# A cosine transform moved from 64x64 to 128x32 column tiles, and transposes written as four 128x32 matmuls, in a block-matching filter kernel

## Chip, cores and metric

The kernel runs on one core of one Trainium2 chip. The metric is the time of one execution on the device in microseconds (us), the median of several runs; less is better. A core has five engines with a queue of instructions each: TensorE (PE in the profile, its weight loads PEld), VectorE (DVE), ScalarE (ACT), GpSimd (POOL) and SyncE (SP). The last two issue most of the DMA transfers here. TensorE reads its operands from SBUF (128 partitions) and writes its results to PSUM, where ScalarE and VectorE pick them up.

## What is computed

The input is x of 8 images, 32 channels, 128 x 128 pixels. Layer 0 normalises x in groups, and finds for each pixel, by block matching in a 5 x 5 window, the 8 offsets with the smallest patch distance. It stacks the 8 shifted copies to 256 channels `xb` (channel = 8 c + k). Layer 1 is a 5 x 5 filter on each channel. Cut to what matters:

```python
xb = _patch_match_stack(x)                 # [8, 256, 128, 128]
dct = _conv(xb, dct_w, groups=C)           # 8 channels in, 8 out, per c
h = relu(_conv(_conv(xb, w1), w2, groups=CK, pad=1))
h = relu(_conv(_conv(h, w3), w4, groups=CK, pad=1))
wiener = sigmoid(_conv(_conv(h, w5), w6, groups=CK, pad=1))
filt = _conv(wiener * dct, inv_dct_w, groups=C)
return _conv(filt, agg_w)
# layer 0: x = x + that(_gn(x));  layer 1: x = x + conv5x5(_gn(x))
```

All data are 32-bit floats. `dct` is the grouped convolution that the change is about: 32 groups of 8 x 8 weights, one product per pixel. It multiplies `wiener` just before the two last 1 x 1 convolutions, which the kernel folds into one matrix `lagg`.

## The kernel before

Each image is cut into 16 strips of 8 rows, and a 17th step finishes the rows that the convolutions' halos left over (136 steps in all). A step runs four stages in the order 3, 2, 1, 0: stages 1 to 3 are the three pairs of a 1 x 1 convolution (`pointwise_v`, `pointwise_t`) and a 3 x 3 depthwise one (`depthwise_v` on VectorE, `depthwise_t` on TensorE), each one strip further behind; stage 0 is the end of a strip: cosine transform, product with `wiener`, `lagg` matmuls (`final_dct`, `final_add`). Between them the step issues a share of the gather for a later strip (`gather_load`, `gather_select`, `gather_pixels`) and of the block matching and statistics of the next image, which wait in the task queues D, A, P, Q and B. How much of the D queue (VectorE's) a step takes is set by costs written into the code (`yield "D", 1.85`) and the function `tick`. The order of instructions on TensorE, VectorE and ScalarE is the order of the program; on GpSimd and SyncE the framework's scheduler puts the transfers into an order of its own when the kernel is built.

What the change and the steps after it touch:

- `final_load` (L770): for strip n it loads four pieces of x (`xr`, L781) and the gathered pixels `xf` back from DRAM (`xbd`, written by L640), all issued by GpSimd. The 256 channels are split over two halves m of 128 partitions. `xf` has one buffer, so its transfers wait until the matmuls of the strip before have read it. The partition order is made by the transfers: eight of them (m, h, g), 32 partitions and 4 KB a row each.
- `mixes` (L300): builds `ldct`, the block-diagonal weights of the cosine transform, [128, 2, 64], from 32 small loads `dq` (L308), once at the start.
- `final_dct` (L796): for each block of four rows (512 columns) and both m, two matmuls with 64 rows of contraction and 64 output partitions each. The four of a block fill the four 64x64 quadrants of the array. Results `pc` lie in two PSUM buffers; VectorE multiplies them into `acc` (L818).
- `ps_x` (L72): a ring of five PSUM buffers, which `pc`, the results of `pointwise_v` (`pv`, L670), `pointwise_t` (`p`, L694), the gather (`pg`, L631), `lagg` (`pa`, L831) and the transposes share. A matmul into a buffer waits until the engine that read it before is done.
- The other large matmuls use 128x32 tiles: 32 output partitions each, four in a row at output partitions 0, 32, 64 and 96 (`pw`, L751, the depthwise stage; `pv`, `p`, `pg`, `pa`). Some use other shapes: the 5 x 5 filter of layer 1 (L924, 64x64), group sums (L255, L264) and the weight preparation (128x128).
- Transposes of 128 x 128 on TensorE with an identity matrix `ident`, in the transpose form of the instruction: `px` in `sources` (L407, 32 per image, before the gather source `xtd` is written by 30 transfers, L424), `pt` in `costs` (L525, 32 per image), `pi` in `places` (L569, 8 per image), and 14 in the setup.
- `gather_load` (L584): GpSimd loads the index rows `ib` (L602), three buffers; ScalarE turns them into selection matrices `sel` (L616, L617) that the `pg` matmuls use.
- `depthwise_v` (L711): eight VectorE instructions per stage and strip (L725), VectorE's largest group.

Of the kernel before, what the change touches and what calls it, by code (L numbers as in the profile page):

```python
# [8 lines left out]
F32 = mybir.dt.float32  # L9
# [7 lines left out]
P = 128  # L17
C, K, H, W = 32, 8, 128, 128
# [18 lines left out]
C_M32 = C_G2 + 32  # L37
# [7 lines left out]
def bm3d_conv_preact(  # L45
# [16 lines left out]
    nc = tc.nc  # L62
    NB = x.shape[0]

    const = ctx.enter_context(tc.tile_pool(name="const", bufs=1))
    keep = ctx.enter_context(tc.tile_pool(name="keep", bufs=1))
    xnp = ctx.enter_context(tc.tile_pool(name="xn", bufs=1))
    work = ctx.enter_context(tc.tile_pool(name="work", bufs=2))
# [29 lines left out]
    cst = const.tile([P, C_N], F32, name="cst")  # L98
    nc.sync.dma_start(cst, consts)
    ident = cst[:, C_ID : C_ID + P]  # L100
# [3 lines left out]
    lw5 = const.tile([P, 2, CK], F32, name="lw5")  # L104


    ldct = const.tile([P, 2, 64], F32, name="ldct")
    lagg = const.tile([P, 2, C], F32, name="lagg")


# [89 lines left out]

    queues = {"B": deque(), "D": deque(), "A": deque(), "P": deque(), "Q": deque()}

# [94 lines left out]
    def mixes():  # L300

        dq = work.tile([P, 2, K], F32, name="dq", tag="dq", bufs=1)
        src = dct_w.rearrange("(m h c i) k a b -> m h k c (i a b)", m=2, h=2, i=K)
        for k in range(K):
            for m in range(2):
                for h in range(2):
                    p = 64 * h + 32 * (k % 2) + 8 * (k // 2)
                    nc.sync.dma_start(dq[p : p + 8, m], src[m, (h + m + 1) % 2, k])  # L308
        m8 = work.tile([P, 8], F32, name="m8", tag="m16", bufs=1)
        yield "D", 1.0, 10  # L310
        nc.vector.tensor_reduce(
            m8,
            cst[:, C_M32 : C_M32 + C].rearrange("p (a c) -> p c a", c=8),
            axis=mybir.AxisListType.X,
            op=ALU.add,
        )
        for m in range(2):
            nc.vector.tensor_tensor(
                ldct[:, m].rearrange("p (c i) -> p c i", i=K),
                m8.unsqueeze(2).to_broadcast([P, 8, K]),  # L320
                dq[:, m].unsqueeze(1).to_broadcast([P, 8, K]),
                ALU.mult,
            )

        iv = work.tile([P, 2, K], F32, name="iv", tag="iv", bufs=1)
        nc.sync.dma_start(iv, inv_w.rearrange("(m p) k a b -> p m (k a b)", p=P))
        ag = work.tile([C, CK], F32, name="ag", tag="xr")
        nc.sync.dma_start(ag, agg_w.rearrange("c i a b -> c (i a b)"))
        for m in range(2):
            yield "D", 0.5  # L330
            ib = work.tile([P, P], F32, name=f"ib_{m}", tag="xm")
            nc.vector.tensor_tensor(
                ib.rearrange("p (c k) -> p c k", k=K),
                cst[:, C_M16 : C_M16 + 16].unsqueeze(2).to_broadcast([P, 16, K]),
                iv[:, m].unsqueeze(1).to_broadcast([P, 16, K]),
                ALU.mult,
            )
            yield "P", 0
            ps = ps_x.tile([P, 512], F32, name=f"ps_ag_{m}", tag="x")[:, :C]
            nc.tensor.transpose(ps, ag[:, m * P : (m + 1) * P], ident[:C, :C])  # L340
            agt = work.tile([P, C], F32, name=f"agt_{m}", tag="agt")
            nc.scalar.copy(agt, ps)
            yield "P", 0
            ps2 = ps_x.tile([P, 512], F32, name=f"ps_ia_{m}", tag="x")[:, :C]
            nc.tensor.matmul(ps2, ib, agt, start=True, stop=True)
            nc.scalar.copy(lagg[:, m], ps2)
# [52 lines left out]
    def sources(b, xn):  # L399


        xl = dram.tile([H, W, C], F32, name=f"xl_{b}", tag="xl")
        for r in range(0, 32, 4):
            yield "P", 0
            pt = ps_x.tile([P, 4, P], F32, name=f"px_{b}_{r}", tag="x")
            for q in range(4):
                nc.tensor.transpose(pt[:, q], xn[:, 3 + r + q, 2 : 2 + W], ident)  # L407
            xs = work.tile([P, 4, P], F32, name=f"xs_{b}_{r}", tag="ct")
            nc.scalar.copy(xs, pt)
            for q in range(4):  # L410
                nc.gpsimd.dma_start(
                    xl.rearrange("(g r) x c -> r x g c", g=4)[r + q],
                    xs[:, q].rearrange("p (g c) -> p g c", c=C),
                )
        xt = xtd[b] = dram.tile([H, QW, NT, C], F32, name=f"xtd_{b}", tag="xtd")
        for j in range(QW):
            for f in range(2):
                ta, tz = f * (NT // 2), (f + 1) * (NT // 2)
                if j < 2 and f == 0:
                    ta += 1  # L420
                if HW * f + TW * (NT // 2 - 1) + j - 2 >= W:
                    tz -= 1
                xa = HW * f + TW * (ta - f * (NT // 2)) + j - 2
                nc.gpsimd.dma_start(  # L424
                    xt[:, j, ta:tz], xl[:, xa : xa + TW * (tz - ta - 1) + 1 : TW]
                )
        jz = W + 2 - HW - TW * (NT // 2 - 1)
        for ja, jz, t, at in ((0, 2, 0, 0), (jz, QW, NT - 1, W - 1)):
            nc.gpsimd.dma_start(
                xt[:, ja:jz, t], xl[:, at : at + 1].to_broadcast([H, jz - ja, C])  # L430
            )
# [53 lines left out]
    def costs(b, i, sq, idx):  # L485
# [35 lines left out]
        for h in range(0, R, 4):  # L521
            yield "P", 0
            pt = ps_x.tile([P, 4, P], F32, name=f"pt_{b}_{i}_{h}", tag="x")
            for q in range(4):
                nc.tensor.transpose(pt[:, q], cost[:, h + q], ident)  # L525
            if h:
                held.clear()
            ct = work.tile([P, 4, P], F32, name=f"ct_{b}_{i}_{h}", tag="ct")
            nc.scalar.copy(ct[:, :, 0 : 4 * NO], pt[:, :, 0 : 4 * NO])
            mx = work.tile([P, 16, K], F32, name=f"mx_{b}_{i}_{h}", tag="mx")  # L530
            for q in range(4):
                yield "D", 1.85
                y = 8 * i + h + q
                for rg in range(4):
                    c25 = ct[:, q, rg : rg + 4 * NO - 3 : 4]
                    nc.vector.max(mx[:, 4 * q + rg], c25)  # L536
                    nc.vector.max_index(  # L537
                        idx[:, rg, y // 4, :, y % 4], mx[:, 4 * q + rg], c25
                    )
        push(places(b, idx, i))  # L540

    def places(b, idx, i):
# [23 lines left out]
        yield "P", 0  # L566
        for h in range(2):
            pt = ps_x.tile([P, 512], F32, name=f"pi_{b}_{i}_{h}", tag="x")
            nc.tensor.transpose(pt[:, :P], o[:, h * P : (h + 1) * P], ident)  # L569
            li = work.tile([P, P], U8, name=f"li_{b}_{i}_{h}", tag="li")  # L570
            nc.scalar.copy(li, pt[:, :P])
            for f in range(2):
                nc.gpsimd.dma_start(
                    idxd[b][i, 4 * h : 4 * h + 4, f],
                    li[:, HW * f : HW * (f + 1)],
                )
# [193 lines left out]
    def final_load(b, n):  # L770
        j0, j1 = (3, R) if n == 0 else (0, R if n < NS else 3)
        ya, yz = R * n - 3 + j0, R * n - 3 + j1

        whole = j1 - j0 == R
        nr, nw = (2, W) if whole else (j1 - j0, C)
        xr = work.tile([P, 2 * W], F32, name=f"xr_{b}_{n}", tag="xr")
        xr = xr[:, : nr * nw].rearrange("p (r w) -> p r w", w=nw)
        for j in range(4):
            ra = ya + 2 * j if whole else ya
            xa = 0 if whole else C * j  # L780
            nc.gpsimd.dma_start(  # L781
                xr[C * j : C * (j + 1)], x[b, :, ra : ra + nr, xa : xa + nw]
            )

        xf = xbp.tile([P, 2, R, W], F32, name=f"xf_{b}_{n}", tag="xf", bufs=1)
        src = xbd[b].rearrange("(j m h c) g y x -> g m h j c y x", j=4, m=2, h=2)
        for m in range(2):
            for h in range(2):
                for g in range(2):
                    p = 64 * h + C * g  # L790
                    nc.gpsimd.dma_start(  # L791
                        xf[p : p + C, m, j0:j1], src[g, m, (h + m + 1) % 2, :, :, ya:yz]
                    )
        return xr, xf, j0, j1

    def final_dct(b, n, acc, xf, j0, j1):  # L796

        for r0 in range(0, R, 4):
# [5 lines left out]
            pc = [  # L804
                ps_x.tile([P, 4, W], F32, name=f"pc_{b}_{n}_{m}_{r0}", tag="x") for m in range(2)
            ]
            for h in range(2):
                for m in range(2):
                    o = 64 * ((h + m + 1) % 2)
                    nc.tensor.matmul(  # L810
                        pc[m][o : o + 64, : z - a],
                        ldct[64 * h : 64 * h + 64, m],
                        xf[64 * h : 64 * h + 64, m, a:z],
                        start=True,
                        stop=True,
                    )
# [362 lines left out]
```

## Time and profile before

| | |
|---|---|
| median of 3 runs | 6524.21 us (6519.26 to 6526.59) |
| the profiled execution: its time | 6526.97 us |
| the profiled execution: first to last instruction (span) | 6525.2 us |
| mean granted TensorE clock | 0.979 of full speed |
| TensorE: `pc` (L810), all forms | 2112 records, 64x64, 128 to 512 columns |
| TensorE: `px`, `pt`, `pi` (L407, L525, L569) | 256, 256 and 64 records, 128x128; 272, 272 and 327 ns median each |
| VectorE: depthwise (L725) | 3264 instructions, 4031.6 us |
| VectorE: `pc` product (L818) | 528 instructions, 679 ns median |
| GpSimd: issues of `xf` (L791) | 1088, 651.0 us, 632 ns each; 180.6 us of waiting for `pc` before them |
| GpSimd: issues of `ib` (L602) | 512, 570 ns each; 1207.3 us of waiting before them |
| from issue to landing, median | `xf` of 128 KB 6.8 us, `ib` 4.0 us |

How to read it: an engine's share of busy time is a mean over stages with different limits. TensorE's records overlap: the next matmul starts while the last one's results still run out, so four records of 590 ns in four column tiles occupy the array together for about 430 ns, and the time that a row of matmuls takes is read from start to start. An fp32 matmul leaves two records (two passes), a transpose one. The chain of waits is followed back from the last instruction; where it passes through an engine, that engine's work set the time there. What the profile calls a line is the line of the program that issued the instruction.

### The profile page before, as it was taken

How to read it: one execution, taken by the hardware profiler on the slowest of the kernel's cores; microseconds unless marked ns; L12 is line 12 of the kernel's file. 1: busy time of each engine (PE TensorE's matmuls, PEld its weight loads, DVE VectorE, ACT ScalarE, POOL GpSimd, SP SyncE). 2: the span in 40 equal slices, each digit the busy share in tenths (PEclk: the TensorE clock that was granted, in tenths of full speed). 3: DMA queues.
4: the chain of work that ended last, by engine and by line, in shares of the span. 5: the costliest groups of instructions: out<-in, count | busy, mean ns of one | idle time of the engine just before them, and what ended most of it. 6: DMA issues, size and time to landing. Idle time of an engine off the chain costs nothing.

```text
span 6525.2 us, 234180 instructions
## 1 busy us (share of the span) xinstructions
PE 6180.3 (95%) x102306; PEld 3262.3 (50%) x102306; DVE 5856.5 (90%) x8828; ACT 5051.0 (77%) x6698; POOL 3077.3 (47%) x5015
## 2 busy tenths in 40 slices
PE   5799999999999999999999999999999999999997
PEld 1445445544555546454555544544545454465553
DVE  7899988999889998899998999899998999988776
ACT  5787769778787877877778787887869787787772
POOL 8345436444364444643446534454345644344334
PEclk7899999999999999999999999999999999999998
DMA  4555555565555655655546556565555665455553
GB/s 85 125 135 144 123 124 146 145 143 135 133 145 139 142 147 127 150 140 135 141 129 157 140 131 151 127 150 137 139 134 138 150 147 133 118 149 147 137 135 79
DMA packets 544960, 886.21 MB, mean 136 GB/s; under 512 B 248880, under 2 KB 312944, under 8 KB 543936
## 3 DMA queue, kind: packets, MB, share of 16 engines
q0 software_dynamic: 383648, 611.87, 37.4%
q1 hardware_dynamic: 157776, 258.11, 16.4%
q8 instruction: 805, 13.19, 0.9%
q10 hardware_dynamic: 2512, 1.25, 0.1%
q14 instruction: 219, 1.79, 0.1%
HBM read 420.60 MB, written 216.49 MB: 98 GB/s over the span
## 4 chain that ended last, share of the span: by engine, by line
PE 50%; DVE 32%; ACT 5%; POOL 5%; DMA 4%; issue 4%; SPq 0%; ACTq 0%; DVEq 0%; POOLq 0%
DVE acc L725 21%; PE pw L751 16%; PE pv L670 12%; PE p L694 11%; PE pg L631 4%; DVE idx L537 3%; POOL xtd L424 3%; PE pc L810 2%; DVE df L444 2%; DVE acc L818 1%; PE p L924 1%; DVE mx L536 1%; PE pd L459 1%; DMA t<-t 1%; ACT sel L616 1%
## 5 line engine op out<-in xcount | busy, mean ns | idle before, releaser
L725 DVE SCALAR_TENSOR_TENSOR acc<-tv,dwv,acc 128x1024 f32<-128x1024 f32 (+3 forms) x3264 | 4031.6, 1237 | 156.3 <-ACT acc L722 52.0
L751 PE MATMUL pw<-t,dwd 96*32 96x254 f32 (+7 forms) x31680 | 2118.1, 419 | 23.0 <-DMA t<-t 10.1
L751 PEld LDWEIGHTS pw<-t,dwd 96*32 96x32 f32 (+1 forms) x31680 | 1105.7, 110 | 826.8 <-issue 369.3
L616 ACT ACTIVATE sel<-ib,nplace 128x1024 f32<-128x1024 uint8 x1024 | 1170.8, 1143 | 62.0 <-DMA ib<-idxd 62.0
L617 ACT ACTIVATE sel<-sel 128x1024 f32<-128x1024 f32 x1024 | 1086.0, 1061 | 32.5
L670 PE MATMUL pv<-acc,lw 128*32 128x512 f32 x8448 | 959.8, 590 | 54.4 <-DVE acc L818 47.8
L694 PE MATMUL p<-acc,lw 128*32 128x256 f32 x16768 | 974.3, 379 | 2.2 <-issue 2.2
L602 POOL DMA_DIRECT2D ib<-idxd x512 | 292.0, 570 | 1207.3 <-ACT sel L616 1078.1
L791 POOL DMA_DIRECT2D xf<-xbd x1088 | 651.0, 632 | 279.9 <-PE pc L810 180.6
L694 PEld LDWEIGHTS p<-acc,lw 128*32 128x32 f32 x16768 | 570.7, 111 | 393.6 <-issue 67.4
L729 ACT ACTIVATE acc<-acc 128x1024 f32<-128x1024 f32 (+3 forms) x408 | 417.1, 1022 | 390.2 <-DVE acc L725 389.8
L678 ACT COPY tv<-pv 128x512 f32<-128x512 f32 (+2 forms) x784 | 435.9, 579 | 338.5 <-PE pv L670 334.1
L631 PE MATMUL pg<-sel,xt 120*32 120x88 f32 (+1 forms) x24576 | 611.7, 244 | 64.8 <-ACT sel L617 56.1
L631 PEld LDWEIGHTS pg<-sel,xt 120*32 120x32 f32 x24576 | 559.5, 111 | 219.2 <-ACT sel L617 74.4
L670 PEld LDWEIGHTS pv<-acc,lw 128*32 128x32 f32 x8448 | 290.2, 110 | 532.3 <-issue 409.7
L764 ACT ACTIVATE acc<-pw 128x512 f32<-128x512 f32 (+2 forms) x808 | 436.6, 572 | 133.4 <-PE pw L751 131.8
L444 DVE TENSOR_TENSOR df<-xn 128x786 f32<-128x786 f32 (+2 forms) x576 | 530.4, 972 | 2.2 <-PE pd L459 1.9
L701 ACT COPY t<-p 128x512 f32<-128x512 f32 x800 | 421.7, 571 | 115.4 <-PE p L694 115.4
L452 ACT ACTIVATE df<-df 128x786 f32<-128x786 f32 (+2 forms) x576 | 458.9, 859 | 50.0 <-DVE df L444 48.6
L722 ACT ACTIVATE acc<-tv,dwv 128x1024 f32<-128x1024 f32 (+3 forms) x408 | 455.1, 1115 | 42.3 <-PE pa L831 24.8
L670 PE MATMUL pv<-xb,lw 128*32 128x512 f32 x4096 | 470.8, 596 | 0.0
L694 PE MATMUL p<-xb,lw 128*32 128x256 f32 x8192 | 469.9, 380 | 0.0
(155 smaller groups left out, 5893.0 us busy)
## 6 DMA issues: line engine op xcount, KB each, us to landing
ib<-idxd POOLq DMA_DIRECT2D x512, 256.0 KB, 4.0
xbd<-xb POOLq DMA_DIRECT2D x128, 1024.0 KB, 6.0
xf<-xbd POOLq DMA_DIRECT2D x960, 128.0 KB, 6.8
t<-t SPq DMA_DIRECT2D x792, 128.0 KB
t<-t SPq DMA_DIRECT2D x384, 256.0 KB
tv<-tv SPq DMA_DIRECT2D x384, 130.0 KB
xt<-xtd POOLq DMA_DIRECT2D x240, 180.0 KB, 4.0
xtd<-xl POOLq DMA_DIRECT2D x192, 96.0 KB, 3.3
```

What stands on the lines that cost most here:

```text
L444: nc.vector.tensor_sub(df[:, :, ca:cz], xn[:, r0 : r0 + SR, ca:cz], xn[:, r0 + dy : r0 + dy + SR, ca + dx : cz + dx],)
L452: nc.scalar.activation(df[:, :, ca:cz], df[:, :, ca:cz], AF.Square)
L616: nc.scalar.activation(sel, ib, AF.Square, bias=nplace)
L617: nc.scalar.activation(sel, sel, AF.Relu, scale=-1.0, bias=1.0)
L631: nc.tensor.matmul(pg[C * j : C * (j + 1), :, :, xa:xz], xt[: 8 * QW, f * (NT // 2) + t], sels[j // 2][: 8 * QW, j % 2 * 2 : j % 2 * 2 + 2 ...
L670: nc.tensor.matmul(ps[C * j : C * (j + 1), :hr], lhsT[:, g, P + C * j : P + C * (j + 1)], src(g)[:, h : h + hr], start=g == 0, stop=g == 1,)
L694: nc.tensor.matmul(ps[C * r : C * (r + 1), e, :nb], lhsT[:, g, s], rows[:, r : r + 4 * nb - 3 : 4], start=g == 0, stop=g == 1,)
L722: nc.scalar.activation(acc, rows, AF.Copy, scale=tap)
L725: nc.vector.scalar_tensor_tensor(acc, rows, tap, acc, op0=ALU.mult, op1=ALU.add)
L751: nc.tensor.matmul(pt[u][C * j : C * (j + 1), ka:kz, :nb, xa:xz], dwd[0:hi, i - 1, u, j, dx + 1], t[0:hi, j, ka:kz, :nb, xa + dx : xz + dx ...
L764: nc.scalar.activation(rows[:, u : u + 2 * nh[u] - 1 : 2, :nb], pt[u][:, : nh[u], :nb], funcs[i - 1])
L791: nc.gpsimd.dma_start(xf[p : p + C, m, j0:j1], src[g, m, (h + m + 1) % 2, :, :, ya:yz])
```

## The change

`ldct` becomes 128 columns wide per half, and its partition order becomes the natural one (j, c, g) of `xbd`, so that `xf` arrives by two transfers of 128 partitions instead of eight of 32. `final_dct` issues eight matmuls per block, each with all 128 rows and 32 output partitions, of which most weights are zeros: an output tile q uses the columns 32 q to 32 q + 32 of `ldct`. All transposes of `px`, `pt` and `pi` go through a new function that issues four ordinary matmuls of 128x32, with the data as weights and the identity as the moving operand. The transposes of the setup stay.

```diff
-    ldct = const.tile([P, 2, 64], F32, name="ldct")
+    ldct = const.tile([P, 2, P], F32, name="ldct")
...
+    def transpose(out_, in_):
+        for j in range(0, P, C):
+            nc.tensor.matmul(out_[j : j + C], in_[:, j : j + C], ident, start=True, stop=True)
...
-        src = dct_w.rearrange("(m h c i) k a b -> m h k c (i a b)", m=2, h=2, i=K)
+        src = dct_w.rearrange("(m c i) k a b -> m k c (i a b)", m=2, i=K)
         for k in range(K):
             for m in range(2):
-                for h in range(2):
-                    p = 64 * h + 32 * (k % 2) + 8 * (k // 2)
-                    nc.sync.dma_start(dq[p : p + 8, m], src[m, (h + m + 1) % 2, k])
-        m8 = work.tile([P, 8], F32, name="m8", tag="m16", bufs=1)
+                p = 32 * (k // 2) + k % 2
+                nc.sync.dma_start(dq[p : p + 31 : 2, m], src[m, k])
+        m16 = work.tile([P, 16], F32, name="m16", tag="m16", bufs=1)
...
-            cst[:, C_M32 : C_M32 + C].rearrange("p (a c) -> p c a", c=8),
+            cst[:, C_M32 : C_M32 + C].rearrange("p (c g) -> p c g", g=2),
...
-                m8.unsqueeze(2).to_broadcast([P, 8, K]),
-                dq[:, m].unsqueeze(1).to_broadcast([P, 8, K]),
+                m16.unsqueeze(2).to_broadcast([P, 16, K]),
+                dq[:, m].unsqueeze(1).to_broadcast([P, 16, K]),
...
-                nc.tensor.transpose(pt[:, q], xn[:, 3 + r + q, 2 : 2 + W], ident)
+                transpose(pt[:, q], xn[:, 3 + r + q, 2 : 2 + W])
...
-                nc.tensor.transpose(pt[:, q], cost[:, h + q], ident)
+                transpose(pt[:, q], cost[:, h + q])
...
-            nc.tensor.transpose(pt[:, :P], o[:, h * P : (h + 1) * P], ident)
+            transpose(pt[:, :P], o[:, h * P : (h + 1) * P])
...
-        src = xbd[b].rearrange("(j m h c) g y x -> g m h j c y x", j=4, m=2, h=2)
+        src = xbd[b].rearrange("(j m c) g y x -> m j (c g) (y x)", j=4, m=2)
         for m in range(2):
-            for h in range(2):
-                for g in range(2):
-                    p = 64 * h + C * g
-                    nc.gpsimd.dma_start(
-                        xf[p : p + C, m, j0:j1], src[g, m, (h + m + 1) % 2, :, :, ya:yz]
-                    )
+            nc.gpsimd.dma_start(
+                xf[:, m, j0:j1].rearrange("p y x -> p (y x)"), src[m, :, :, W * ya : W * yz]
+            )
...
-            for h in range(2):
-                for m in range(2):
-                    o = 64 * ((h + m + 1) % 2)
+            for m in range(2):
+                for q in range(4):
+                    s = slice(C * q, C * (q + 1))
                     nc.tensor.matmul(
-                        pc[m][o : o + 64, : z - a],
-                        ldct[64 * h : 64 * h + 64, m],
-                        xf[64 * h : 64 * h + 64, m, a:z],
+                        pc[m][s, : z - a],
+                        ldct[:, m, s],
+                        xf[:, m, a:z],
```

## The prediction

> **What bounds the kernel now.** I read the page's shares and chain first, then TensorE's timeline in a late stretch, then busy times of single steps, then the chain where GpSimd appears in it.
>
> ```profile
> span 6525.2 us, 234180 instructions
> PE 6180.3 (95%) x102306; PEld 3262.3 (50%) x102306; DVE 5856.5 (90%) x8828; ACT 5051.0 (77%) x6698; POOL 3077.3 (47%) x5015
> ...
> PE 50%; DVE 32%; ACT 5%; POOL 5%; DMA 4%; issue 4%; SPq 0%; ACTq 0%; DVEq 0%; POOLq 0%
> ```
>
> TensorE is nearly full, VectorE almost as full, and the chain changes sides between them. So work added to TensorE costs its full length in some steps and nothing in others. The change adds TensorE work, and the question is how many steps pay.
>
> The price comes from one step of the last image (start, start to end, form, records; each fp32 matmul leaves two records):
>
> ```profile
> 6220.44 1.04 PE L751 MATMUL pw<-t,dwd 128*32 128x508 f32 x8
> 6221.41 1.95 PE L810 MATMUL pc<-xf,ldct 64*64 64x512 f32 x16
> 6223.29 1.16 PE L631 MATMUL pg<-sel,xt 120*32 120x88 f32 x48
> ...
> 6229.42 3.62 PE L670 MATMUL pv<-acc,lw 128*32 128x512 f32 x32
> 6232.85 1.06 PE L831 MATMUL pa<-acc,lagg 128*32 128x256 f32 x16
> 6233.72 3.65 PE L694 MATMUL p<-acc,lw 128*32 128x256 f32 x64
> 6237.17 1.14 PE L631 MATMUL pg<-sel,xt 120*32 120x88 f32 x48
> 6238.12 3.62 PE L670 MATMUL pv<-acc,lw 128*32 128x512 f32 x32
> ```
>
> Ends overlap the next start, so I count from start to start. 32 records of 128x32 by 512 columns take 6232.85 - 6229.42 = 3.43 us (107 ns each, four column tiles side by side), 64 records by 256 columns 6237.17 - 6233.72 = 3.45 (54 ns), 48 by 88 columns 6238.12 - 6237.17 = 0.95 (20 ns). The cosine product takes 6223.29 - 6221.41 = 1.88 us for 16 records; its four 64x64 tiles also run together. It is entered late: the eight `pw` records should take 8 x 0.107 = 0.85 and take 0.97.
>
> **The cosine product.** A full strip has two blocks of four rows. Before: 0.97 + 1.88 = 2.85 us from the `pw` records to `pg`. After: eight matmuls per block, 32 records of exactly the `pv` form, so 0.85 + 3.43 = 4.28. That is +1.43 us per strip, the vanished changes of tile shape already in it: the records' own price rises by 1.72 (16 x 107 ns) and about 0.28 of entry and exit goes. The first strip of an image has 640 columns instead of 1024 and the last 384, which gives +0.8 and +0.36. An image pays 15 x 1.43 + 1.2 = 22.7, eight images 182 us of TensorE time, 1.33 per strip on average.
>
> The page "TensorEngine Tiling (Array Packing)" of the Trainium skill speaks against the change: under Theoretical Speedup it gives up to 2x where a dimension is at most 64, and the change fills the rows up to 128 with zeros. By that rule the product would take 2 x 1.88 = 3.76 us instead of the 3.43 that the `pv` rows give, and the sum would be, as an estimate, 45 us larger if all 136 strips paid; the rows decide, because the 1.88 holds the entry and exit that go.
>
> **Who pays.** I cut the trace at each strip's first `pc` record into 135 steps and took TensorE's time without streaming (gaps over 0.16 us, so that changes of shape do not count) and VectorE's idle time in each. Three steps, one of each kind (sum and mean of the answer left out):
>
> ```profile
> core 0: us, PE busy (x) PEld busy (x) DVE busy (x) ACT busy (x) POOL busy (x), PEclk, DMA share, GB/s
> 6221.40:6264.20 42.80, 42.80 (x758) 23.11 (x754) 33.99 (x31) 34.93 (x44) 12.60 (x23) 1.00 0.53 137
> 3868.70:3916.00 47.30, 45.09 (x773) 22.01 (x772) 45.90 (x85) 38.40 (x52) 18.39 (x32) 1.00 0.56 138
> 3470.60:3519.10 48.50, 47.34 (x803) 23.32 (x803) 42.58 (x46) 38.34 (x52) 40.85 (x57) 1.00 0.66 161
> ```
>
> - TensorE alone sets the pace (first row: it is never idle, VectorE idles 8.8 us): 50 steps, all of the last image's full strips among them. Each pays: 50 x 1.33 = **+67 us**.
> - VectorE sets the pace (second row, 1.4 us idle): 31 steps, TensorE waiting 129 us in them, 4.2 each, mostly `pv` for the `pc` buffers that VectorE has yet to read (L670 after L818). The longer product goes into this wait. What is left: VectorE's product for the second half can start 0.86 us later than for the first, while one product takes 0.68 (median of L818), so two blocks lose at most 2 x 0.18 = 0.35. Between 0 and 11 us, I take **+5**.
> - Both wait (53 steps). In about 21 of them, three in each of seven images, GpSimd's queue is what is late (next part), and I count nothing. Of the other 32: the chain of waits runs through 65 groups of `pc` records (114 us), so at least 65 - 50 = 15 pay, since lengthened parts of a path lengthen it; at most 32. Middle 24 x 1.33 = **+32 us** (20 to 43).
>
> If the cover in the second kind is gone, it costs 31 x 1.33 = 41 us.
>
> **The loads of `xf`.** Eight transfers of 32 partitions become two of 128, the bytes stay. GpSimd's queue loses 1088 - 272 = 816 issues of 632 ns; I price a 128-partition issue like L602's 570 ns or L640's 716 ns, so about the same per issue. On GpSimd this is 516 us, but it waits most of its time for others (L602 alone sat idle 1207 us before it) and only counts where its queue is late. That is once per image, behind the 30 `xtd` transfers:
>
> ```profile
> 3478.73 22.40 POOL xtd L424 x28
> ...
> 3507.78 1.56 POOL xf L791 x3
> 3509.34 0.06 issue
> 3509.39 1.69 POOL xf L791 x3
> 3511.08 8.24 DMA ib<-idxd
> 3519.32 0.02 issue
> 3519.35 1.16 ACT sel L616
> ```
>
> ScalarE waits for `ib`, which stands behind six `xf` issues. In the built order of the changed kernel one `xf` transfer stands there, so 5 x 0.63 = 3.1 us go, in seven images **-22 us** (0 if VectorE takes over, -44 if the earlier arrival also shortens the 8.24 us). The next thing late there is ScalarE's selection for `pg`. The order of instructions on TensorE, VectorE and ScalarE stays otherwise the same; on GpSimd's and SP's queues neighbours swap places, for which I have no price and add 10 us to each side. The waiting first `xf` transfer holds the queue until the last `pc` record as before, 1.4 us later, with `xbd` and `ib` behind it; `ib` has three buffers, which is the cover.
>
> **The transposes.** 64 groups of four for `pt`, 64 for `px`, 32 pairs for `pi`. One before: `pt` starts at 3021.75, the next `p` at 3022.34, so 0.59 us, entered about 0.14 late and with 0.02 lost behind. After: 32 records by 128 columns. No clean row has this width; between 20 ns (88 columns) and 54 ns (256) it is 0.64 to 1.73 us per group, and on the line between them 28 ns or 0.9. Against 0.59 + 0.16 this is +0.15 per group, 128 groups +19, pairs about 0. None lies in the last image, and most are in steps that wait for VectorE or GpSimd: I take a third, **+6 us** (-5 to +45).
>
> The setup (16 small loads fewer on SP, two wider products) ends long before the first use of `ldct` at 288 us; nothing, and at most 16 x 0.7 us of SP queue, hidden by the 25 us `xtd` block.
>
> **Sum.** 67 + 5 + 32 - 22 + 6 = +88 us on the profiled execution's 6526.97 (span 6525.2), which lies 2.8 above the median 6524.21. On the median: 6612; rounded, **6612 us**.
>
> **Rivals.**
> 1. *Every strip pays.* VectorE has idle time too (566 us over these steps), so its steps may stretch with TensorE's as both wait in turn. For it: 90% and 95% busy leave no room for reordering. Against: 4.2 us of TensorE wait per VectorE step. 182 + 19 - 22 = +179: 6703 us.
> 2. *Mostly hidden.* Only the last image's 17 strips (23 us) pay, with a few others (20). For it: the chain is PE only half of the time; against: 50 steps with no TensorE wait. With -22: +21, 6545 us.
> 3. *Faster: GpSimd's queue.* Price: all `xf` on the chain, 30 us of issues and 55 us of landings, disappears, and the earlier `ib` hides all strips but the last image's: 23 - 85 = -62, 6462 us. It decides if the steps behind the queue are worth more than the 67 us of steps in which GpSimd is idle two thirds of the time. Against: such steps are about 21 of 135.
> 4. *Not what it says:* the four 128x32 tiles do not run side by side with this data. The `pv` records have the same form and do; I give it nothing.
>
> **Chances and range.** What a measurement can tell from no change is about 0.2%, 13 us. My forecast (+35 to +140) 0.72; rival 1 (+140 and over) 0.15; rival 2 (up to +35) 0.10, of it 0.03 within 13 us; rival 3 0.03. Faster 0.03, same 0.03, slower 0.94. The low ends (67 + 0 + 20 - 44 - 5 - 10) give +28; the high end needs most strips to pay. Range 6555 to 6695.
>
> **What would show it.** Right: the last image's steps 44.2 us instead of 42.8; `pc` groups of 3.4 us; no delay at entry to `pc` and `pt`; VectorE-bound steps such as the one from 3868.7 still about 47.3 with a shorter TensorE wait; `xf` issues 272. Wrong: the VectorE-bound steps also longer by 1.4 (rival 1), or the step behind `xtd` shorter by more than 4 us (rival 3), or records by 128 columns over 40 ns.

## The result, and the profile after

| | before | after |
|---|---|---|
| median | 6523.57 us (6519.26 to 6526.59, 4 runs) | 6681.24 us (6665.97 to 6690.72, 4 runs) |
| ratio, 95% interval | | 1.024 (1.022 to 1.026) |
| profiled execution: time, span | 6526.97, 6525.2 us | 6690.72, 6688.9 us |

The changed kernel is slower by 158 us; 88 were forecast. Its profiled execution lies 9.5 us above its median, so sums over steps of the trace come out somewhat larger than the medians say. The page's span, shares and chain of the changed kernel:

```profile
span 6688.9 us, 245335 instructions
PE 6357.4 (95%) x108450; PEld 3759.9 (56%) x108450; DVE 5863.7 (88%) x8828; ACT 5065.8 (76%) x6698; POOL 2648.3 (40%) x4199
...
PE 65%; DVE 15%; DMA 7%; ACT 5%; issue 4%; POOL 3%; SPq 0%; ACTq 0%; DVEq 0%; POOLq 0%
```

TensorE's part of the chain rose from 50% to 65%, VectorE's fell from 32% to 15%: steps in which VectorE set the pace are now near TensorE's length. But DMA rose too, from 4% to 7%, and that was in no step of the forecast.

TensorE's timeline in the last image of the changed kernel (start, start to end, form, records):

```profile
6406.91 5.33 PE L754 MATMUL pw<-t,dwd 96*32 96x512 f32 x48
6412.04 3.63 PE L810 MATMUL pc<-xf,ldct 128*32 128x512 f32 x32
6415.47 1.14 PE L634 MATMUL pg<-sel,xt 120*32 120x88 f32 x48
```

The product takes 6415.47 - 6412.04 = 3.43 us for 32 records, as the `pv` rows said, and nothing is lost ahead of it any more. The three steps of the forecast again, in the changed kernel (busy time of each engine in each stretch):

```profile
core 0: us, PE busy (x) PEld busy (x) DVE busy (x) ACT busy (x) POOL busy (x), PEclk, DMA share, GB/s
6412.04:6456.20 44.16, 44.16 (x772) 24.50 (x768) 33.96 (x31) 34.92 (x44) 12.88 (x24) 1.00 0.49 133
3952.40:3999.80 47.40, 46.64 (x828) 25.48 (x822) 46.00 (x85) 38.45 (x52) 15.23 (x26) 1.00 0.55 139
3595.20:3657.90 62.70, 54.62 (x871) 30.19 (x867) 52.13 (x81) 47.04 (x61) 32.08 (x49) 0.95 0.64 152
```

The first is the step of the last image, 42.8 before and 44.2 now. The second is the step that began at 3868.7 and is set by VectorE: 47.3 before, 47.4 now. Both are as forecast. The third is the step behind the `xtd` block: its counterpart, cut at the `pc` records, took 59.5 us before and takes 62.7 now, where the forecast had it about 3 us shorter. What is late there shows in the chain of waits and in the timeline of GpSimd:

```profile
3586.47 14.76 DMA ib<-idxd
3601.23 0.02 issue
3601.25 1.16 ACT sel L619
```

```profile
3582.01 1.46 POOL L432 DMA_DIRECT2D xtd<-xl  x2
3583.46 1.69 POOL L477 DMA_DIRECT2D sq<-sm  x3
3585.14 0.74 POOL L643 DMA_DIRECT2D xbd<-xb  x1
3585.77 0.83 POOL L791 DMA_DIRECT2D xf<-xbd  x1
3586.47 0.71 POOL L605 DMA_DIRECT2D ib<-idxd  x1
```

As forecast, one `xf` issue stands ahead of `ib` instead of six, and `ib` is issued soon after the `xtd` block. But it takes 14.76 us to land instead of 8.24. The page's DMA issues (KB of each transfer, median us from issue to landing) and the waits of the engines tell the same of the whole run:

```profile
ib<-idxd POOLq DMA_DIRECT2D x512, 256.0 KB, 4.4
xbd<-xb POOLq DMA_DIRECT2D x128, 1024.0 KB, 14.3
xf<-xbd POOLq DMA_DIRECT2D x240, 512.0 KB, 13.1
t<-t SPq DMA_DIRECT2D x792, 128.0 KB, 4.5
```

```profile
ACT sel L619 <- DMA ib<-idxd: 90.2, 14, 13.1
PE pw L754 <- DMA t<-t: 33.6, 16, 7.1
PE pc L810 <- DMA xf<-xbd: 24.3, 7, 4.7
POOL x1d L844 <- DMA xf<-xbd: 89.5, 17, 15.1
```

An `xf` transfer lands 13.1 us after its issue (6.8 before, with a quarter of the bytes), and `xbd`, which writes 1 MB next to it, after 14.3 (6.0 before). The waits (us in total, times, longest) grew with them: ScalarE's for `ib` from 62.0 to 90.2, TensorE's for the halo rows `t` from 10.1 to 33.6 and for `xf` itself from 0.8 to 24.3, GpSimd's `x1d` for `xf` from 54.3 to 89.5.

### The profile page after: what moved, and what is told of

It reads as the page before. It is cut to its first block, busy times and chain, and to the rows that moved or that the text cites. A ratio compares the mean times of both kernels' runs of the same rounds, so it can differ in the third digit from the quotient of the medians.

```text
span 6688.9 us, 245335 instructions
## 1 busy us (share of the span) xinstructions
PE 6357.4 (95%) x108450; PEld 3759.9 (56%) x108450; DVE 5863.7 (88%) x8828; ACT 5065.8 (76%) x6698; POOL 2648.3 (40%) x4199
## 4 chain that ended last, share of the span: by engine, by line
PE 65%; DVE 15%; DMA 7%; ACT 5%; issue 4%; POOL 3%; SPq 0%; ACTq 0%; DVEq 0%; POOLq 0%
PE pw L754 22%; PE pv L673 15%; PE p L697 14%; DVE acc L728 9%; PE pg L634 5%; PE pc L810 5%; DMA t<-t 2%; DMA ib<-idxd 2%; DVE idx L540 2%; POOL xtd L427 2%; PE p L924 2%; PE pd L462 1%; DMA xf<-xbd 1%; PE pa L831 1%; ACT df L455 1%
## 5 line engine op out<-in xcount | busy, mean ns | idle before, releaser
L754 PE MATMUL pw<-t,dwd 128*32 128x254 f32 (+7 forms) x31680 | 2135.9, 419 | 54.9 <-DMA t<-t 33.6
L754 PEld LDWEIGHTS pw<-t,dwd 96*32 96x32 f32 (+1 forms) x31680 | 1215.9, 110 | 758.9 <-issue 342.4
L619 ACT ACTIVATE sel<-ib,nplace 128x1024 f32<-128x1024 uint8 x1024 | 1170.8, 1143 | 90.2 <-DMA ib<-idxd 90.2
L697 PEld LDWEIGHTS p<-acc,lw 128*32 128x32 f32 x16768 | 649.8, 111 | 317.6 <-issue 54.5
L605 POOL DMA_DIRECT2D ib<-idxd x512 | 309.3, 604 | 1034.1 <-ACT sel L619 999.0
L634 PEld LDWEIGHTS pg<-sel,xt 120*32 120x32 f32 x24576 | 594.8, 110 | 162.8 <-issue 56.7
L634 PE MATMUL pg<-sel,xt 120*32 120x88 f32 (+1 forms) x24576 | 625.9, 242 | 49.5 <-ACT sel L620 33.5
L673 PEld LDWEIGHTS pv<-acc,lw 128*32 128x32 f32 x8448 | 340.6, 110 | 443.0 <-issue 352.2
L810 PE MATMUL pc<-xf,ldct 128*32 128x512 f32 (+2 forms) x4224 | 494.7, 599 | 40.4 <-DMA xf<-xbd 24.3
L641 ACT COPY xb<-pg 128x512 f32<-128x512 f32 x512 | 301.0, 588 | 239.2 <-PE pg L634 231.4
L784 POOL DMA_DIRECT2D xr<-in_x_dram x544 | 275.7, 520 | 518.3 <-DVE acc L728 301.3
## 6 DMA issues: line engine op xcount, KB each, us to landing
xbd<-xb POOLq DMA_DIRECT2D x128, 1024.0 KB, 14.3
xf<-xbd POOLq DMA_DIRECT2D x240, 512.0 KB, 13.1
```

Of the source, the lines that this page charges most:

```text
L619: nc.scalar.activation(sel, ib, AF.Square, bias=nplace)
L634: nc.tensor.matmul(pg[C * j : C * (j + 1), :, :, xa:xz], xt[: 8 * QW, f * (NT // 2) + t], sels[j // 2][: 8 * QW, j % 2 * 2 : j % 2 * 2 + 2 ...
L673: nc.tensor.matmul(ps[C * j : C * (j + 1), :hr], lhsT[:, g, P + C * j : P + C * (j + 1)], src(g)[:, h : h + hr], start=g == 0, stop=g == 1,)
L697: nc.tensor.matmul(ps[C * r : C * (r + 1), e, :nb], lhsT[:, g, s], rows[:, r : r + 4 * nb - 3 : 4], start=g == 0, stop=g == 1,)
L754: nc.tensor.matmul(pt[u][C * j : C * (j + 1), ka:kz, :nb, xa:xz], dwd[0:hi, i - 1, u, j, dx + 1], t[0:hi, j, ka:kz, :nb, xa + dx : xz + dx ...
L810: nc.tensor.matmul(pc[m][s, : z - a], ldct[:, m, s], xf[:, m, a:z], start=True, stop=True,)
```

## The experiments

Twelve kernels ran, in four groups, each group beside the kernel before on the same chip; the medians of the kernel before lay between 6525.86 and 6527.89 in these groups, so differences across groups are good to some 4 us (6523.57 beside the changed kernel).

### The parts of the change

The three parts, alone and in pairs. e1: the changed kernel with the old transposes. e2: the kernel before with the new transposes. e3: the changed kernel with `xf` in eight transfers. e5: e1 and e3 together. Where `xf` is in eight transfers:

```diff
-            nc.gpsimd.dma_start(
-                xf[:, m, j0:j1].rearrange("p y x -> p (y x)"), src[m, :, :, W * ya : W * yz]
-            )
+            for j in range(0, 4, 1):
+                nc.gpsimd.dma_start(
+                    xf[C * j : C * (j + 1), m, j0:j1].rearrange("p y x -> p (y x)"),
+                    src[m, j : j + 1, :, W * ya : W * yz],
+                )
```

and where the transposes are the old ones, at all three places:

```diff
-                transpose(pt[:, q], cost[:, h + q])
+                nc.tensor.transpose(pt[:, q], cost[:, h + q], ident)
```

> The changed kernel with the old transposes; the cosine product on 128x32 tiles and the two large xf transfers stay. Theory T (the part of the loss that the prediction missed, about 70 us, comes from xf arriving as two transfers of 512 KB, which other transfers wait behind): 6660 to 6680 us, little below the changed kernel's 6681, because the transposes cost about 6 to 19 us. Rival W (the longer TensorE work is paid in nearly every step, since TensorE and VectorE wait in turn): 6655 to 6675. Rival R (the transposes cost the missing part): 6600 to 6620.

> The kernel before with only the transposes as four 128x32 matmuls. The group of four takes 0.88 us in the changed kernel's trace against 0.59 and about 0.16 of entry and exit before, so +0.13 us for each of 128 groups. Theory T: 6520 to 6540 us. Rival W: all 128 groups pay, about 6540. Rival R: 6580 to 6600.

> The changed kernel with xf in eight transfers of 32 partitions, as before the change, TensorE's work unchanged. Theory T: the missing 70 us go, 6600 to 6630 us, the xf transfers land in about 7 us again and TensorE's waits for t<-t and xf fall to the level of before. Rival W: 6670 to 6690.

> The changed kernel with the old transposes and with xf in eight transfers: only the cosine product's tiles are changed, and the partition order. Theory T: 6595 to 6620 us, the predicted cost of the cosine product alone (+67 +5 +32 = +104 on 6524, 6628 without the shorter GpSimd queue, is the upper end if nothing else changes). Rival W: 6655 to 6675.

| | product | transposes | `xf` transfers | us | ratio (95%) |
|---|---|---|---|---|---|
| e1 | new | old | 2 | 6657.16 | 1.0203 (1.0186 to 1.022) |
| e2 | old | new | 8, as before | 6541.28 | 1.0018 (1.0007 to 1.0028) |
| e3 | new | new | 8 | 6590.24 | 1.0101 (1.0084 to 1.0118) |
| e5 | new | old | 8 | 6580.42 | 1.0086 (1.0069 to 1.0103) |

Eight transfers instead of two are worth 91 us (6681.24 - 6590.24), and 77 without the new transposes (e1 - e5). The transposes cost 10 to 13 us (e3 - e5, e2 against before), and about 24 beside the two large transfers (after - e1, across groups), so the two parts are not independent. Theory R falls with e1. Between T and W, e1 decides nothing, for it lies 3 us under T's range and inside W's; e3 and e5 do: they lie 10 and 15 us under T's ranges, but some 80 and 75 under W's. So the time that the forecast lacks is in the transfers. What about them is not shown by this.

### The size, the form and the queue of the transfers; another tiling

e4 makes four transfers of 64 partitions (the loop of e3 with step 2 and two entries of j), e8 eight of 128 partitions and two image rows, e9 moves the two large ones to SP's queue (`nc.sync.dma_start`). e7 is another question: the product on 32x32 tiles, in the kernel before.

```diff
-            nc.gpsimd.dma_start(
-                xf[:, m, j0:j1].rearrange("p y x -> p (y x)"), src[m, :, :, W * ya : W * yz]
-            )
+            for r in range(j0, j1, 2):
+                rz = min(r + 2, j1)
+                nc.gpsimd.dma_start(
+                    xf[:, m, r:rz].rearrange("p y x -> p (y x)"),
+                    src[m, :, :, W * (ya + r - j0) : W * (ya + rz - j0)],
+                )
```

That is e8; of e7 the matmuls:

```diff
-            for h in range(2):
-                for m in range(2):
-                    o = 64 * ((h + m + 1) % 2)
+            for m in range(2):
+                for q in range(4):
+                    s, o = slice(C * q, C * (q + 1)), C * ((q + m) % 4)
...
-                        pc[m][o : o + 64, : z - a],
-                        ldct[64 * h : 64 * h + 64, m],
-                        xf[64 * h : 64 * h + 64, m, a:z],
+                        pc[m][o : o + C, : z - a],
+                        ldct[s, m],
+                        xf[s, m, a:z],
```

> The changed kernel with xf in four transfers of 64 partitions (256 KB each) in place of two of 128 (512 KB). Two transfers gave 6681 us, eight of 32 partitions 6590. Theory S (the size of one transfer: it lands late, and GpSimd's in-order queue, in which later transfers wait for the landing of earlier ones, is held that long): between the two, about 6620 to 6650, and the median time from issue to landing between 5.5 and 13.1 us. Theory A (only the step from two transfers to more matters, for example because two leave a fixed part of the path without work): 6590 already.

> The changed kernel with xf in eight transfers again, but each of 128 partitions and two image rows (128 KB) in place of 32 partitions and eight rows. Theory S (the size of one transfer decides): near the 6590 us of eight transfers of 32 partitions, up to 6605, landing times near 6 us. Theory P (a transfer over 128 partitions is the slow form, whatever its size): stays near 6681, with landing times of 9 us and more.

> The changed kernel with its two xf transfers of 512 KB issued by SP in place of GpSimd; size, form and bytes unchanged. Theory Q (the cost is GpSimd's queue, held behind the late landings: x1d, dsum's, xn and xt transfers stand behind it): the waits of GpSimd's transfers for xf vanish and the time falls below 6640 us, unless SP's queue, held in the same way, delays the t<-t transfers that TensorE's pw waits for, which the waits before pw would show. Theory B (the two large transfers take the DMA engines from whoever else needs them, whichever queue issues them): stays at 6670 to 6700.

> The kernel before with the cosine product on 32x32 tiles: eight matmuls per block on eight different tiles of the array (no zeros in the weights outside an 8 by 8 block pattern of 32 rows), old transposes, eight xf transfers of 32 partitions and 128 KB. TensorE's product took 1.88 us per strip on 64x64 tiles (16 records) and 3.43 on 128x32 (32 records). Theory X (tiles in different rows and columns run side by side): 32 records of 32x32 in about 1.0 to 1.9 us, and by the 53 us that 1.4 us more per strip cost, at best 35 us less than before: 6490 to 6525. Theory Y (tiles of one column share its output and run one after the other): 3.4 us per strip, so about 6580, as with 128x32 tiles and eight transfers.

| | us | ratio (95%) |
|---|---|---|
| e4 | 6715.59 | 1.0291 (1.0271 to 1.031) |
| e8 | 6619.57 | 1.0143 (1.0123 to 1.0163) |
| e9 | 6699.65 | 1.0272 (1.0254 to 1.0289) |
| e7 | 6532.93 | 1.0014 (1.0005 to 1.0024) |

Theory S fell with e4, and A with it: half the size, and slower than the changed kernel by 34 us. Its transfers land after the same time as those of twice their size (page of e4):

```profile
xf<-xbd POOLq DMA_DIRECT2D x480, 256.0 KB, 13.0
```

Theory P fell with e8, which lies 62 us below the changed kernel though its transfers span 128 partitions; but it lies 29 above e3 and 15 above the range that S gave it. e9 did not tell Q from B: GpSimd's waits for `xf` are gone, but the wait that Q named as its exception is there (waits of TensorE in e9):

```profile
PE pw L754 <- DMA t<-t: 99.3, 35, 6.4
```

What these runs have in common shows in the trace's records of single DMA packets. I counted how many were in progress at once, every 50 ns from 10 to 14 us after each strip's first `xf` issue, when a quick load is over. In the kernel before, e3 and e8 no number from 2 to 14 has over 7% of the counts. In the changed kernel about 27% are exactly 8 and 16% are 9, in e4 some 25% and 17%, and in e9 36% are exactly 4 and 15% are 5. I take it that in the slow kernels a part of the 16 DMA engines is still busy when the rest has finished: 8 in the changed kernel and e4, 4 in e9. The records do not name a packet's engine, and counts of up to 23 occur, so a count is not strictly a number of engines.

This has a reading that fits them. The rows of `xf` are (j, c, g), and the source of a transfer has j as its outermost dimension, with 4 entries, 2 in e4; in e3 one transfer holds one j, and its outermost dimension is (c g) with 32. If so many engines share a transfer, up to 16, then two transfers of 512 KB lie on 4 engines each and four of 256 KB on 2 each, 8 engines and 128 KB per engine in both. 128 KB are 32 packets of 4 KB; at 246 ns each (their mean on GpSimd's queue in the changed kernel's trace) one engine needs 7.9 us for them, and 2.0 us for the 32 KB of the kernel before (four engines to 128 KB). The difference, 5.9 us, is near the 13.1 - 6.8 = 6.3 that landing grew. e8 keeps 32 KB on each of four engines and lands in 6.4 us; e3 has 8 KB on each of sixteen and lands in 5.5. The order in which the source is read is not the cause: e3 reads it in the order of the changed kernel and is quick. What the reading leaves open is why e4, with the same 128 KB per engine, is 34 us slower than the changed kernel.

A page of the Trainium skill states such a rule: "DMA: Bandwidth & Descriptors", in "Why a DMA increments its semaphore by 16 and not by 1", says that a transfer goes to the largest number of engines, at most 16, that divides the slowest dimension (other than 1) of its source and of its destination, apart from some copies on GpSimd's queue; on GpSimd's queue to the next ones in turn and on SP's always to the lowest-numbered. The counts agree: 8 packets in progress, 4 + 4, for two transfers from GpSimd, and 4 for two from SP. That the 4 from SP are the same engines fits this, but no record names them.

e7 met theory X at its upper end in TensorE's time for the product; the median, 6532.93, lies above the 6525 that X gave at most. TensorE's timeline in e7:

```profile
6226.26 1.95 PE L809 MATMUL pc<-xf,ldct 32*32 32x512 f32 x32
6228.14 1.16 PE L631 MATMUL pg<-sel,xt 120*32 120x88 f32 x48
```

32 records in 1.88 us, just what 16 records on 64x64 tiles take: records follow each other at half the distance (59 ns for 117), but the product needs twice as many. So no time of TensorE is won. The median is 6 us above before; the steps together are 7.9 us shorter, but the first `pc` record comes 13.2 us later, for TensorE waits 13.0 us in the setup for `ag`, which is loaded on SP behind 64 small loads in place of 32.

### The same transfers on 16 engines

e10 changes nothing of the changed kernel but the order of the rows: (c, g, j) in place of (j, c, g). The two transfers of 512 KB stay. e11 does it to the kernel before, with four transfers of 256 KB.

```diff
-                p = 32 * (k // 2) + k % 2
-                nc.sync.dma_start(dq[p : p + 31 : 2, m], src[m, k])
+                p = 4 * (k % 2) + k // 2
+                nc.sync.dma_start(dq[p : p + 121 : 8, m], src[m, k])
...
-        src = xbd[b].rearrange("(j m c) g y x -> m j (c g) (y x)", j=4, m=2)
+        src = xbd[b].rearrange("(j m c) g y x -> m (c g) j (y x)", j=4, m=2)
```

(The mask `m16` follows.) In e11:

```diff
-        src = xbd[b].rearrange("(j m h c) g y x -> g m h j c y x", j=4, m=2, h=2)
+        src = xbd[b].rearrange("(j m h c) g y x -> m h (c g) j (y x)", j=4, m=2, h=2)
...
-                for g in range(2):
-                    p = 64 * h + C * g
-                    nc.gpsimd.dma_start(
-                        xf[p : p + C, m, j0:j1], src[g, m, (h + m + 1) % 2, :, :, ya:yz]
-                    )
+                nc.gpsimd.dma_start(
+                    xf[64 * h : 64 * (h + 1), m, j0:j1].rearrange("p y x -> p (y x)"),
+                    src[m, (h + m + 1) % 2, :, :, W * ya : W * yz],
+                )
```

> The changed kernel, again with two xf transfers of 128 partitions and 512 KB on GpSimd's queue, but the rows of ldct and xf in the order (c, g, j) in place of (j, c, g), so that the outermost dimension of the source has 32 entries and not 4. Four transfers of 256 KB (6716 us) were slower than two of 512 KB (6681), and in both about half of the DMA engines stayed busy 10 to 14 us after the first issue; so theory S, that the size of one transfer decides, has fallen. Theory E (the number of engines that share a transfer is set by the outermost dimension of the source: 4 engines for two transfers of 512 KB, 2 for four of 256 KB, 16 for the eight of 32 partitions that gave 6590): landing falls from 13.1 us to 8 or less, the stretch with half of the engines busy vanishes, and the time is 6575 to 6615. Theory N (few large transfers are slow in themselves, by what stands behind them in GpSimd's queue): stays above 6650.

> The kernel before, product on 64x64 tiles and old transposes, with xf in four transfers of 64 partitions and 256 KB in place of eight of 32 and 128 KB, rows in the order (h, c, g, j): the outermost dimension of the source has 16 entries, not 4. Theory E (engines per transfer) sees 128 KB on 4 engines (32 KB an engine, landing 6.8 us) become 256 KB on 16 (16 KB an engine): landing 5 to 7 us, half of the issues gone; faster than before by 10 to 40 us, 6487 to 6517. Theory H (landing at 6.8 us is hidden already in the kernel before, and its cost begins only beyond that): within 10 us of before, 6517 to 6537.

e10: 6575.30 us, ratio 1.0075 (1.0059 to 1.009), 106 us less than the changed kernel. e11: 6503.99 us, ratio 0.9965 (0.9951 to 0.9979), 23 us less than the kernel before. The DMA issues in e10:

```profile
xbd<-xb POOLq DMA_DIRECT2D x128, 1024.0 KB, 7.2
xf<-xbd POOLq DMA_DIRECT2D x240, 512.0 KB, 5.7
```

Same size, same form at the destination, same queue, same number: 5.7 us instead of 13.1, and `xbd` beside them 7.2 instead of 14.3. The counts of exactly 8 or 9 packets, some 43% in the changed kernel, are 5% here. The waits that had grown are short (e10), and TensorE's for `xf` itself is gone:

```profile
ACT sel L613 <- DMA ib<-idxd: 33.1, 14, 7.0
PE pw L748 <- DMA t<-t: 4.6, 4, 2.8
POOL x1d L838 <- DMA xf<-xbd: 5.7, 7, 1.2
```

Theory E holds, N falls, and with e11 also H: 6.8 us was not yet hidden. But KB per engine do not order the quick loads: by E, 32 KB an engine landed in 6.8 us (before), 6.4 (e8) and 5.7 (e10), and 16 KB in 6.1 (e11). The step behind the `xtd` block in e10, on GpSimd and on ScalarE (in brackets the idle time before, and what ended it):

```profile
3523.56 0.72 POOL L785 DMA_DIRECT2D xf<-xbd  x1
3524.13 0.71 POOL L599 DMA_DIRECT2D ib<-idxd  x1
```

```profile
3531.60 1.15 ACT L613 ACTIVATE sel<-ib,nplace 128x1024 f32<-128x1024 uint8 x1 [2.57 <-DMA ib<-idxd]
```

ScalarE's in the changed kernel:

```profile
3601.25 1.15 ACT L619 ACTIVATE sel<-ib,nplace 128x1024 f32<-128x1024 uint8 x1 [12.71 <-DMA ib<-idxd]
```

The issues stand in the same order in both. From the issue of `ib` to ScalarE's start it is 7.5 us in e10 and 14.8 in the changed kernel. The step, cut at the `pc` records, takes 52.6 us in e10 against 62.7.

### The product alone, and issues against engines

e12 is e10 with the old transposes. e13 is e11 with each transfer cut in two by image rows, so that there are eight issues of 128 KB again:

```diff
-                nc.gpsimd.dma_start(
-                    xf[64 * h : 64 * (h + 1), m, j0:j1].rearrange("p y x -> p (y x)"),
-                    src[m, (h + m + 1) % 2, :, :, W * ya : W * yz],
-                )
+                for r, rz in ((j0, min(j1, 4)), (4, j1)):
+                    if rz > r:
+                        nc.gpsimd.dma_start(
+                            xf[64 * h : 64 * (h + 1), m, r:rz].rearrange("p y x -> p (y x)"),
+                            src[m, (h + m + 1) % 2, :, :, W * (ya + r - j0) : W * (ya + rz - j0)],
+                        )
```

> The product on 128x32 tiles alone, with the two quick xf transfers of 512 KB (rows in the order (c, g, j)) and the old transposes. Against the kernel before with four quick transfers (6504 us) it holds what the product alone costs. Theory C (steps in which TensorE alone sets the pace pay 1.4 to 1.5 us, 50 of them, and no others): 6504 + 50 to 75 = 6555 to 6575, and 5 to 15 below the 6575 of the same kernel with the new transposes. Theory D (as forecast, about 24 of the steps that wait for both also pay): 6504 + 104 = 6608.

> The kernel before with the rows of xf in the order (h, c, g, j) and xf in eight transfers of 64 partitions and four image rows (128 KB, 16 entries in the outermost dimension of the source): as many issues as before, of the same size, on 16 engines in place of 4. Four such transfers of 256 KB gave 6504, the kernel before 6527. Theory E (the engines per transfer bring the gain): 6495 to 6512. Theory I (half as many issues on GpSimd's queue bring it): 6517 to 6537.

e12: 6563.83 us, ratio 1.0058 (1.0044 to 1.0071). It is 59.8 above e11 and 11.5 below e10: theory C, not D. e13: 6506.90 us, ratio 0.9972 (0.9962 to 0.9982), 3 us from e11: in the kernel before it is the engines, not the number of issues.

In the changed kernel the number does count. e5 and e12 differ in it (eight transfers, two) and in the order of the rows, and by theory E both use 16 engines: e12 is 16.6 us faster, and with the new transposes e10 is 14.9 faster than e3. Since e12 has two transfers where e11 has four, 59.8 is the product's price together with that; with eight on both sides it is 73.5 (e5 - e13). So the product alone costs 60 to 74 us, which is theory C's range by either way.

## Why the prediction was right and where it was wrong

The sign was right and the time lay in the range, but 6612 came from two errors that partly cancel. The forecast had +104 for the product (67 + 5 + 32), -22 for the loads of `xf` and +6 for the transposes. By the runs, the change is made of: -23.5 for `xf` if it used 16 engines, in four transfers (e11), +59.8 product, with two transfers for four (e12 - e11), +11.5 transposes (e10 - e12), +105.9 for the order of the rows by which, after theory E, two transfers use 4 engines each (after - e10). The sum is 154 of the 158; as differences along one way it had to come out, and the missing 4 lie between the groups. So the loads cost about 82 us (105.9 - 23.5) where a gain of 22 was forecast, and the product about 60 where 104 was. That the time fell into the range was luck: with the product at the forecast's price, the loads as they are would have made it some 6725, above the range's 6695.

I cut the traces again at each strip's first `pc` record and kept the kinds that the steps had before (134 of the 135 steps, as in the forecast):

| kind of step | forecast | product, and two quick transfers for four (e11 to e12) | as built (before to after) |
|---|---|---|---|
| TensorE alone sets the pace, 50 | +67 | +69.8, median 1.40 | +89.4, median 1.50 |
| VectorE sets the pace, 31 | +5 | 0.0 | -31.7 |
| both wait, 53 | +32 and -22 | -17.8 | +104.0 |
| of these, the seven behind the `xtd` blocks | -22 | -22.0 | +37.0 |

The -22.0 is not the product's own: with eight quick transfers on both sides (e13 to e5) these seven steps grow by 13.4 us. The other steps together grow by 67 there and by 74 from e11 to e12, nearly all of it where TensorE alone sets the pace.

- *The price of the product.* 3.43 us per strip, 1.4 us per step of the last image: right to 0.1 us.
- *TensorE alone sets the pace.* Right: 67 forecast, 69.8 measured with quick transfers.
- *VectorE sets the pace.* Right: +5 forecast, 0.0 measured; the longer product went into TensorE's wait (in the step from 3868.7, 47.30 - 45.09 = 2.2 us not busy before, 47.40 - 46.64 = 0.8 now). This is what rival 1 denied, so its 6703, the rival's time nearest to the result, was near for another reason. The -31.7 as built is hardly a gain: the five of these steps that shorten most (3.5 to 6.1 us) each follow a step that is 3.2 to 8.4 us longer. Against e10, the changed kernel loses 131 us in 20 steps that are each over 2 us longer, and six others give back 27.
- *Both wait.* Wrong: "Middle 24 x 1.33 = +32 us". Without the seven steps behind `xtd`, the 46 others grew by 4.2 us together (-17.8 + 22.0). The faulty reasoning was "so at least 65 - 50 = 15 pay, since lengthened parts of a path lengthen it". That a chain passes through a piece does not show how far it can grow at the cost of waits elsewhere in the step; by the 4.2 us, nearly all of it was taken up. Which waits took it was not followed.
- *The loads of `xf`.* This is the step that failed: "Eight transfers of 32 partitions become two of 128, the bytes stay", priced by the issues alone, -22. The mechanism that it named is there: where eight transfers become two and both are quick (e5 to e12), the seven steps behind the `xtd` blocks are 29.3 us shorter, near the 22, and the time 16.6. But, by theory E, the loads went from 4 engines for 128 KB to 4 engines for 512 KB, and I had given landing times no price. In the seven steps that alone makes +70.2 (e10 to after), where ScalarE's selection waits for an `ib` that lands late; that `ib` shares engines with `xf` and `xbd` is the likely reason, but no record names its engines. 13 more steps lose 2 to 8 us each. Which wait is the last one in each of those 13 I did not settle; TensorE's waits for `t` (10.1 to 33.6 us) and for `xf` (0.8 to 24.3) are candidates. It is the same for the forecast's "`ib` has three buffers, which is the cover": the cover is against a late issue, not against a late landing.
- *The transposes.* The price was right (0.877 us for a group of four, 0.9 forecast; 27.4 ns a record, 28 forecast). That "a third" of the 19 us is paid was too little: 10 to 13 us were, and about 24 beside the slow transfers.
- *Rival 3*, faster through GpSimd's queue, was not wild in its size: with 16 engines the loads gain 23 us in the time (e11), and the seven steps are 32 us shorter from before to e12, product included. But the 23 come from the engines and not from fewer issues (e13), which the rival named. And they do not outweigh the product's 60.

## A version that beats both

e11, the kernel before with its rows in the order (h, c, g, j): 6503.99 us, 0.35% below before (0.21 to 0.49%) and 2.7% below the changed kernel.

## What to carry to other kernels

Before transfers are merged, look at the outermost dimension of their source as well as at their number and bytes: here 4 entries instead of 32 made the same two transfers land in 13.1 instead of 5.7 us and cost 106 us, and the page's median landing of the kernel before (6.8 us for 128 KB, 5.4 in e13) was already a sign of it. Time added to TensorE was paid in full in the steps where TensorE never waits, and little elsewhere; the share of the chain overstated it. Where a change has several parts, vary one with the others held, for two wrong prices of opposite sign can look like a good forecast.

## What the runs showed that was not expected

- Transfers issued from GpSimd with a source of 4 outer entries left 8 DMA packets in progress at once for two transfers, those issued from SP only 4.
- Thirty-two fp32 records on 32x32 tiles take the 1.88 us of sixteen on 64x64 tiles (59 and 117 ns each).
- 64 instead of 32 tiny weight loads on SP moved the first `pc` record from 288 us by 13.2 us, through a wait of TensorE in the setup. In the changed kernel, with 16 fewer, it comes 1.8 us earlier.
